# A four-layer graph network: the fourth layer's first products in one bf16 pass, its range sums by bf16 thirds, its vector products in one operation

## The chip, the core and the metric

One core of a Trainium2 chip runs the whole network in one launch. The metric is the device time of that launch in microseconds (us), the median of several runs. Before the change it is 19,167.42 us (three runs, 19,167.29 to 19,172.29).

## What is computed

The network has 12,500 nodes with 32 features (8 scalars and 8 vectors of 3) and 400,000 edges, sorted by target. Each of four layers normalizes the node features, sends messages along the edges and adds what arrives at each target to the features. The change concerns the fourth layer:

```python
h = jax.nn.relu(edge_scalars @ (fc_w1 * (1.0 / np.sqrt(NUM_BASIS)))) * SQRT2      # 8 -> 256
w = (h @ (fc_w2 * (1.0 / np.sqrt(HIDDEN)))).reshape(E, 4, MUL, MUL)               # 256 -> 4 x 8 x 8
x = node_features[edge_src]
s1 = x[:, :MUL]
v1 = x[:, MUL:].reshape(E, MUL, 3)
s2 = edge_sh[:, 0]
v2 = edge_sh[:, 1:4]
out_s = A_SCALAR * (jnp.einsum('eu,euw->ew', s1 * s2[:, None], w[:, 0]) + INV_SQRT3 * jnp.einsum('eui,ei,euw->ew', v1, v2, w[:, 1]))
out_v = A_VECTOR * INV_SQRT3 * (jnp.einsum('eu,euw,ei->ewi', s1, w[:, 2], v2) + jnp.einsum('eui,euw->ewi', v1 * s2[:, None, None], w[:, 3]))
edge_features = jnp.concatenate([out_s, out_v.reshape(E, 3 * MUL)], axis=1)
node_out = jax.ops.segment_sum(edge_features, edge_dst, num_segments=N)
```

Every edge has a small network of its own scalars (8, then 256, then 256 values), whose result weights the features of the edge's source; the weighted sums are added up by target.

## The kernel before

The edges are cut into windows of 2,048: 16 columns of 128 edges, 196 windows in all. Since the edges are sorted by target, the targets of a window span fewer than 128 nodes, so the sums of a window form one tile of 128 nodes by 32 features (this is the path named fast; another one, for inputs where that does not hold, is chosen at run time and not taken here). Layer 0 runs from 0 to about 5.1 ms, layers 1 and 2 together from 5.15 to 16.23 ms, and the fourth layer, `edges3`, from 16.33 to 23.06 ms. Beside layer 0's groups a generator, `rest`, is stepped: it clears the tables, prepares the weights and computes some values by edge.

`edges3` is unrolled over the 196 windows. For a window `c` and four quarters `s` of four columns each:

- `fetch` (called two windows ahead) loads the sources, the places of the targets, `edge_attr_4` and the eight scalars (`emb`, four transfers on SP), and issues 16 gathers on POOL (L1130), one for each column, of the source features `hs`.
- `hidden` (L1140, one window ahead) makes the 256 hidden values: two f32 matmuls for each quarter, with 8 contracted rows and 512 edges each, and a relu on ACT (L1142).
- `scalars` (L1149 to L1152) forms the two scalar inputs `q` on DVE.
- `product` (L1162) makes the 256 weights of each edge: eight matmuls a quarter with 128 hidden rows. An f32 matmul is recorded as two passes. Then DVE multiplies out of PSUM: `pa` (L1167, 512 elements) and four times `pb` (L1172, 256 elements each).
- `places` makes the one-hot matrix `oh` of each column on ACT (L1194, L1195).
- `outputs` (L1178 to L1188), for the window before, reduces `pa` and `pb` on DVE, multiplies by `edge_attr_4` and adds, into `f` (32 values an edge).
- `collect` (L1201) sums `f` by target with 16 f32 matmuls; four columns run in four column groups of PE, so four partial sums of 32 rows come out. ACT copies them (L1204), and `add` folds the four into one (L1207), which ACT copies (L1209) and `put` writes to one of two tables (SP).

Each engine works off its own list in order. The lists follow the Python code, but a scheduler may let an instruction pass others: PE takes, after a quarter's product, collect of the window before, then hidden, fold and the other quarters between them; DVE takes the two large reduces ahead of the next window's quarter 0. The PSUM tiles of the weights (`pw3`) have two buffers, so PE can be two quarters ahead of DVE. At the end `gather_sum` adds the tables (two for this layer) to the features.

Of the kernel before, what the change touches and what calls it, by code (L numbers as in the profile page):

```python
# [16 lines left out]
P = 128  # L17
# [9 lines left out]
NTAB = 4  # L27
ROUND = 12582912.0
# [7 lines left out]
class GNN:  # L36
# [14 lines left out]
    def __init__(self, tc, ctx, a, out, E):  # L51
# [15 lines left out]

        self.mid = dram.tile([rows, D + 1], F32, name="mid", tag="mid")
# [10 lines left out]
    def setup(self):  # L79
# [48 lines left out]
        self.w1q = keep.tile([P, 256], F32, name="w1q")  # L128
        self.w2b = keep.tile([P, 2, 256], F32, name="w2b")

    def weights(self, pool):
# [47 lines left out]
        nc.vector.memset(self.w1q, 0.0)  # L179
        for q in range(Q4):  # L180
            nc.scalar.dma_start(self.w1q[32 * q : 32 * q + 8], self.a["L3_gnn_fc_w1"])
        nc.vector.tensor_scalar_mul(self.w1q, self.w1q, math.sqrt(2.0) / math.sqrt(8.0))
# [14 lines left out]
    def rest(self, pool):  # L197
# [4 lines left out]
        for l in range(4):  # L202
            for t in self.tabs[l][:2] if self.fast and l != 2 else self.tabs[l]:
                self.clear(t, zero)
                yield
        yield from self.weights(pool)
        if self.fast:
            yield from self.places_by_edge(pool)
            yield from self.unit_vectors(pool)

# [100 lines left out]

    def clear(self, t, zero):
# [50 lines left out]
    def gather_sum(self, l, pool):  # L363
# [3 lines left out]
        for k, t in enumerate(self.tabs[l][: 2 if self.fast and l != 2 else NTAB]):  # L367
# [22 lines left out]

    def get(self, pool, l, c):
# [4 lines left out]
    def put(self, l, c, s):  # L396

        self.nc.sync.dma_start(self.tabs[l][c["no"] % 2][ds(self.first(c), P), :], s)

# [699 lines left out]
    def layer3(self):  # L1099
        nc = self.nc  # L1100
        self.norm_relu(3)
# [5 lines left out]
    def edges3(self):  # L1107

        nc, tc, CT = self.nc, self.tc, self.CT
        IT = CT * CPI1  # L1110
        with ExitStack() as ctx:
            ld = ctx.enter_context(tc.tile_pool(name="load3", bufs=2))
# [6 lines left out]
            def fetch(c, it):  # L1119
                row = it * CPI1 + c["no"]  # L1120
                c["src"] = self.load(gp, "src", c["col"])
                c.update(self.places_of(gp, row))
                c["sh"] = self.load(gp, "edge_attr_4", c["col"])
                c["emb"] = ld.tile([P, B], F32, name="emb")
                for q in range(Q4):
                    nc.sync.dma_start(c["emb"][32 * q : 32 * q + 8],
                                      self.a["ea8_c"][q, :, ds(row, 1), :].rearrange("f o e -> f (o e)"))
# [6 lines left out]
            def hidden(c, m, h):  # L1134
                if (m, h) == (0, 0):
                    c["hid"] = wp.tile([P, 2, CT, Q4, 32], F32, name="hid")
                t = ph.tile([P, 2, B], F32, name="ps_h")
                for q in range(2):
                    r = 32 * (2 * h + q)
                    nc.tensor.matmul(t[:, q, :], lhsT=self.w1q[r : r + 8, m * P : (m + 1) * P],  # L1140
# [248 lines left out]
```

## Time and profile before

| what | value |
|---|---|
| median of three runs | 19,167.42 us |
| the profiled execution | 23,109.4 us |
| its span on the chip | 23,107.7 us |
| mean granted TensorE clock in it | 0.828 of full |
| recorded instructions | 229,565 |
| DMA packets | 1,503,407 |

The profile is of one execution in which every instruction and packet was recorded; it took 3,942 us longer than the median of the runs. PE is TensorE's matmuls, PEld its weight loads, DVE VectorE, ACT ScalarE, POOL GpSimd (which issues the gathers) and SP the engine that issues most transfers. In a row of groups there are the line, the engine, the operation, output and inputs with their shapes and the count, then busy time in us with the mean of one in ns, then the idle time of the engine just before, with what ended it; "issue" means that the engine waited for nothing that the profile shows.

```profile
PE 15954.9 (69%) x74484; PEld 8493.8 (37%) x74484; DVE 11868.8 (51%) x24410; ACT 5515.5 (24%) x12954; POOL 14407.0 (62%) x12552
L1130 POOL DMA_INDIRECT hs<-feat,src x3136 | 3085.0, 984 | 3653.4 <-DVE pb L1172 2657.8
L1162 PE MATMUL ps_w<-w2b,hid 128*128 128x256 f32 x12544 | 4006.1, 462 | 608.6 <-issue 430.0
L1140 PE MATMUL ps_h<-emb,w1q 8*128 8x512 f32 x3136 | 1066.5, 761 | 230.0 <-DMA emb<-in_ea_c 165.1
L1172 DVE TENSOR_TENSOR pb<-ps_w,hs 128x256 f32<-128x256 f32 x3136 | 1281.8, 469 | 0.0
```

Over the whole span PE has the most busy time. In the fourth layer its largest group is the products of L1162.

### The profile page before, as it was taken

What the parts mean: (1) busy time and instruction counts of PE and PEld (TensorE: products, weight loads), DVE (VectorE), ACT (ScalarE), POOL (GpSimd) and SP (SyncE); (2) the same over time, 40 slices, a digit from 0 to 9 for tenths busy, and PEclk for the clock granted to TensorE, in tenths of its full rate; (3) what the DMA queues carried; (4) which work ended last, traced back from release to release, by engine and by line L of the source; (5) the groups of instructions that cost most, each with busy time, mean ns of one, the idle gap of its engine ahead of it and who ended that gap; (6) DMA issues with size and microseconds to landing.
All of it is one profiled execution on the core that took longest, in us unless ns stands there. A gap on an engine that the chain in (4) does not pass through costs nothing.

```text
span 23107.7 us, 229565 instructions
## 1 busy us (share of the span) xinstructions
PE 15954.9 (69%) x74484; PEld 8493.8 (37%) x74484; DVE 11868.8 (51%) x24410; ACT 5515.5 (24%) x12954; POOL 14407.0 (62%) x12552
## 2 busy tenths in 40 slices
PE   2333333328888778778777777787588888888887
PEld 2333333322333333333333333333355445445544
DVE  4443333335555555555555555555455555555555
ACT  0000000002222222222222222222233333333333
POOL 5666666655777777777777777777444444444443
PEclk9999999998777777777777777777687888888887
DMA  2111111113333333333333333333100000000000
GB/s 74 42 35 23 23 23 23 23 40 73 80 80 79 77 78 83 77 78 82 80 78 81 80 77 79 78 83 77 24 12 12 12 12 12 12 12 12 12 12 18
DMA packets 1503407, 1138.52 MB, mean 49 GB/s; under 512 B 1141492, under 2 KB 1304900, under 8 KB 1448308
## 3 DMA queue, kind: packets, MB, share of 16 engines
q1 hardware_dynamic: 745098, 891.46, 12.3%
q0 software_dynamic: 752640, 206.32, 9.7%
q10 hardware_dynamic: 4448, 25.89, 0.3%
q8 instruction: 592, 9.70, 0.2%
q14 instruction: 629, 5.15, 0.1%
HBM read 1022.56 MB, written 99.86 MB: 49 GB/s over the span
## 4 chain that ended last, share of the span: by engine, by line
PE 39%; DVE 18%; another core or an unknown queue 15%; issue 11%; ACT 9%; POOL 5%; DMA 2%; DVEq 0%; SPq 0%; POOLq 0%; ACTq 0%
PE ps_y L746 11%; PE ps_w L1162 10%; PE ps_o L756 4%; PE ps L879 4%; ACT oh L781 3%; DVE z L749 3%; DVE rb L1180 3%; POOL hs L433 2%; DVE pb L1172 2%; PE ps_h L1140 2%; ACT oh L710 2%; PE ps_win L385 2%; PE ps_sum L1201 1%; DVE f L1178 1%
## 5 line engine op out<-in xcount | busy, mean ns | idle before, releaser
L885 POOL DMA_INDIRECT acc<-summed,rows x3136 | 4995.6, 1593 | 1898.0 <-issue 1141.3
L1130 POOL DMA_INDIRECT hs<-feat,src x3136 | 3085.0, 984 | 3653.4 <-DVE pb L1172 2657.8
L1162 PE MATMUL ps_w<-w2b,hid 128*128 128x256 f32 x12544 | 4006.1, 462 | 608.6 <-issue 430.0
L433 POOL DMA_INDIRECT hs<-feat,src x3136 | 3136.5, 1000 | 1881.0 <-issue 864.2
L704 POOL DMA_INDIRECT hs<-feat,src_c x3136 | 3189.0, 1017 | 1126.7 <-issue 932.0
L1162 PEld LDWEIGHTS ps_w<-w2b,hid 128*128 128x128 f32 x12544 | 2722.3, 227 | 2283.9 <-issue 1572.6
L749 DVE TENSOR_TENSOR z<-ps_y,hid 128x1024 f32<-128x1024 f32 x2352 | 2842.0, 1218 | 1235.5 <-PE ps_y L746 1007.3
L385 PE MATMUL ps_win<-m,oh 128*128 128x32 f32 x6272 | 1488.0, 402 | 2521.3 <-ACT m L561 1829.8
L746 PE MATMUL ps_y<-X,w2t 64*128 64x512 f32 x4704 | 2258.9, 838 | 613.4 <-ACT hid L741 306.4
L385 PEld LDWEIGHTS ps_win<-m,oh 128*128 128x128 f32 x6272 | 1398.1, 328 | 2612.4 <-ACT m L561 1921.6
L1167 DVE TENSOR_TENSOR pa<-ps_w,q 128x512 f32<-128x512 f32 x784 | 536.0, 684 | 3153.4 <-PE ps_w L1162 2928.4
L756 PE MATMUL ps_o<-z,sums 128*32 128x512 f32 x9408 | 1936.9, 697 | 2.5 <-issue 1.6
L746 PE MATMUL ps_y<-Q,w2t 64*128 64x512 f32 x4704 | 1688.5, 740 | 83.6 <-DVE z L749 39.8
L723 PE MATMUL ps_m<-eye,hs 128*32 128x128 f32 x6272 | 805.2, 367 | 1048.3 <-ACT X L729 790.5
L879 PEld LDWEIGHTS ps<-hd,eq 128*128 128x128 f32 x6272 | 1048.0, 253 | 1241.9 <-issue 339.4
L879 PE MATMUL ps<-hd,eq 128*128 128x32 f32 x6272 | 1144.2, 335 | 513.7 <-DVE eq L871 197.1
L732 DVE TENSOR_TENSOR Q<-N,X 128x512 f32<-128x512 f32 x392 | 271.6, 693 | 2115.6 <-ACT X L729 1473.0
L1142 ACT ACTIVATE hid<-ps_h 128x1024 f32<-128x1024 f32 x784 | 799.8, 1020 | 2236.2 <-PE ps_h L1140 1651.5
L1172 DVE TENSOR_TENSOR pb<-ps_w,hs 128x256 f32<-128x256 f32 x3136 | 1281.8, 469 | 0.0
L1140 PE MATMUL ps_h<-emb,w1q 8*128 8x512 f32 x3136 | 1066.5, 761 | 230.0 <-DMA emb<-in_ea_c 165.1
L746 PEld LDWEIGHTS ps_y<-X,w2t 64*128 64x128 f32 x4704 | 603.4, 236 | 1658.0 <-issue 742.6
L723 PEld LDWEIGHTS ps_m<-eye,hs 128*32 128x32 f32 x6272 | 546.2, 147 | 1635.2 <-ACT X L729 929.7
(191 smaller groups left out, 18563.7 us busy)
## 6 DMA issues: line engine op xcount, KB each, us to landing
has<-loc_t SPq DMA_DIRECT2D x392, 1024.0 KB
srow<-in_src_t SPq DMA_DIRECT2D x392, 512.0 KB
hs<-feat,src POOLq DMA_INDIRECT x6272
N<-n_t SPq DMA_DIRECT2D x3136, 32.0 KB
edge_attr<-in_edge_attr SPq DMA_DIRECT2D x196, 256.0 KB
hs<-feat,src_c POOLq DMA_INDIRECT x3136
acc<-summed,rows POOLq DMA_INDIRECT x3136
emb<-in_ea_c SPq DMA_DIRECT2D x784, 20.0 KB
```

Source lines behind the costliest of these rows:

```text
L385: nc.tensor.matmul(c["sum"], lhsT=oh[:, k, :], rhs=feat[:, k, :], start=t0 + k == 0, stop=t0 + k == self.CT - 1)
L433: self.nc.gpsimd.indirect_dma_start(out=t[:, k, :], out_offset=None, in_=self.feats[l][:], in_offset=bass.IndirectOffsetOnAxis(ap=idx[:, t ...
L704: nc.gpsimd.indirect_dma_start(out=c["hs"][:, k, :], out_offset=None, in_=self.feats[1][:], in_offset=bass.IndirectOffsetOnAxis(ap=c["src_ ...
L746: nc.tensor.matmul(y[:, q, :], lhsT=self.w2t[64 * q : 64 * q + 64, j, :], rhs=c["Q" if j < 3 else "X"][64 * q : 64 * q + 64, h, :], start= ...
L749: nc.vector.tensor_mul(z, y, c["hid"][:, 2 * h : 2 * h + 2, :])
L756: nc.tensor.matmul(c["o", j // 3][32 * q : 32 * q + 32, :], lhsT=self.sums[:, j, :], rhs=c["z", j, q // 2][:, q % 2, :], start=j % 3 == 0, ...
L879: nc.tensor.matmul(t[:, k, :], lhsT=c["eq"][:, k, :], rhs=c["hd"][:, G * g + k, :], start=True, stop=True)
L885: nc.gpsimd.indirect_dma_start(out=self.tabs[2][k % NTAB][:], out_offset=bass.IndirectOffsetOnAxis(ap=c["rows"][:, G * g + k : G * g + k + ...
L1130: nc.gpsimd.indirect_dma_start(out=c["hs"][:, k, :], out_offset=None, in_=self.feats[3][:], in_offset=bass.IndirectOffsetOnAxis(ap=c["src" ...
L1140: nc.tensor.matmul(t[:, q, :], lhsT=self.w1q[r : r + 8, m * P : (m + 1) * P], rhs=c["emb"][r : r + 8], start=True, stop=True)
L1162: nc.tensor.matmul(w[:, k, :], lhsT=c["hid"][:, m, 4 * g + k].rearrange("p q s -> p (q s)"), rhs=self.w2b[:, m, :], start=m == 0, stop=m == 1)
L1172: nc.vector.tensor_mul(c["pb"][:, i, gs], w[:, :, lo : lo + 64].rearrange("p g (w u) -> p g w u", u=8), by[:, :, None, :].to_broadcast([P, ...
```

## The change

- **First products.** The eight edge scalars are split into three bf16 parts each, whose sum is the f32 value, once for all windows (`parts_of`, stepped in `rest` beside layer 0): each part is written three times to a new tensor in HBM, `emb8`, 57.8 MB in bf16. The weights are split likewise (`stacked`), so that one bf16 matmul with 72 contracted rows makes all nine products of parts. `emb` comes in one transfer of 72 rows by 2,048 edges.
- **Range sums.** `f` is split into three bf16 parts (`thirds`: two copies on ACT, two subtracts on DVE, in turn), `oh` is bf16, and `collect` is 16 bf16 matmuls with 96 columns of weights, one after another, a quarter later than before; the fold runs over 96 rows.
- **Vector products.** The features are stored with the vector components outermost, `vv` holds them multiplied by the scalar of `edge_attr_4`, and `product` makes `pa`, `ps` (256 elements) and `pv` (768 elements, the three components in one operation). `outputs` reduces `pa`, `pv` and `ps`.
- **Around these.** Loads are four windows ahead in six buffers, gathers two ahead as before; the loop of one pass is dropped; `put_late` writes the sums from ACT's queue, with the row number loaded there, to one of four tables instead of two.

```diff
+TABS = {0: 2, 1: 2, 2: 4, 3: 4}
...
+        self.emb8 = dram.tile([9, 8, self.NW, Q4 * B], BF16, name="emb8", tag="emb8")
...
-        self.w1q = keep.tile([P, 256], F32, name="w1q")
+        self.w1s = keep.tile([72, 256], BF16, name="w1s")
...
-        nc.vector.memset(self.w1q, 0.0)
-        for q in range(Q4):
-            nc.scalar.dma_start(self.w1q[32 * q : 32 * q + 8], self.a["L3_gnn_fc_w1"])
-        nc.vector.tensor_scalar_mul(self.w1q, self.w1q, math.sqrt(2.0) / math.sqrt(8.0))
+        self.stacked(pool, self.w1b, self.w1s)
...
-            for t in self.tabs[l][:2] if self.fast and l != 2 else self.tabs[l]:
+            for t in self.tabs[l][: TABS[l]] if self.fast else self.tabs[l]:
...
+            yield from self.parts_of(pool, self.a["ea8_c"], self.emb8)
...
+    def parts_of(self, pool, src, dst):
+        nc = self.nc
+        flat = src.rearrange("f c e -> (f c e)").rearrange("(p e) -> p e", p=P)
+        outs = [dst[k].rearrange("f c e -> (f c e)").rearrange("(p e) -> p e", p=P) for k in range(9)]
+        F = flat.shape[1] // 14
+        for k in range(0, flat.shape[1], F):
+            ks = slice(k, k + F)
+            v = pool.tile([P, 2240], F32, name="pv", bufs=2)[:, :F]
+            nc.sync.dma_start(v, flat[:, ks])
+            yield
+            p = [pool.tile([P, 2240], BF16, name=f"pp{i}")[:, :F] for i in range(3)]
+            nc.scalar.copy(p[0], v)
+            nc.vector.tensor_tensor(v, v, p[0], op=ALU.subtract)
+            yield
+            nc.scalar.copy(p[1], v)
+            nc.vector.tensor_tensor(p[2], v, p[1], op=ALU.subtract)
+            for i in range(3):
+                for j in range(3):
+                    nc.sync.dma_start(outs[3 * i + j][:, ks], p[i])
+            yield
+    def stacked(self, pool, w, out):
+        nc = self.nc
+        f, m = w.shape
+        p = pool.tile([f, 3, m], BF16, name="wp")
+        r = pool.tile([f, m], F32, name="wr")
+        nc.vector.tensor_copy(p[:, 0], w)
+        nc.vector.tensor_tensor(r, w, p[:, 0], op=ALU.subtract)
+        nc.vector.tensor_copy(p[:, 1], r)
+        nc.vector.tensor_tensor(p[:, 2], r, p[:, 1], op=ALU.subtract)
+        for i in range(3):
+            for j in range(3):
+                k = (3 * i + j) * f
+                nc.scalar.dma_start(out[k : k + f], p[:, j])
...
-        for k, t in enumerate(self.tabs[l][: 2 if self.fast and l != 2 else NTAB]):
+        for k, t in enumerate(self.tabs[l][: TABS[l] if self.fast else NTAB]):
...
+    def thirds(self, pool, c, step):
+        nc = self.nc
+        if step == 0:
+            c["f3"] = pool.tile([P, self.CT, 3, D], BF16, name="f3")
+        if step % 2 == 0:
+            nc.scalar.copy(c["f3"][:, :, step // 2, :], c["f"])
+        elif step == 1:
+            nc.vector.tensor_tensor(c["f"], c["f"], c["f3"][:, :, 0, :], op=ALU.subtract)
+        else:
+            nc.vector.tensor_tensor(c["f3"][:, :, 2, :], c["f"], c["f3"][:, :, 1, :], op=ALU.subtract)
...
+    def put_late(self, l, c, s):
+        first = self.nc.values_load(c["wbase"], engines=[mybir.EngineType.Activation], min_val=0, max_val=self.N - 1)
+        self.nc.scalar.dma_start(self.tabs[l][c["no"] % TABS[l]][ds(first, P), :], s)
...
-        self.norm_relu(3)
+        self.norm_relu(3, by_part=self.fast)
...
-            ld = ctx.enter_context(tc.tile_pool(name="load3", bufs=2))
+            ld = ctx.enter_context(tc.tile_pool(name="load3", bufs=6))
...
-            def fetch(c, it):
-                row = it * CPI1 + c["no"]
-                c["src"] = self.load(gp, "src", c["col"])
-                c.update(self.places_of(gp, row))
-                c["sh"] = self.load(gp, "edge_attr_4", c["col"])
-                c["emb"] = ld.tile([P, B], F32, name="emb")
-                for q in range(Q4):
-                    nc.sync.dma_start(c["emb"][32 * q : 32 * q + 8],
-                                      self.a["ea8_c"][q, :, ds(row, 1), :].rearrange("f o e -> f (o e)"))
+            def fetch(c):
+                row = c["no"]
+                c["src"] = self.load(ld, "src", c["col"])
+                c.update(self.places_of(ld, row))
+                c["sh"] = self.load(ld, "edge_attr_4", c["col"])
+                c["emb"] = ld.tile([72, Q4 * B], BF16, name="emb")
+                nc.sync.dma_start(c["emb"], self.emb8[:, :, ds(row, 1), :].rearrange("k f o e -> (k f) (o e)"))
+            def gather(c):
                 c["hs"] = gp.tile([P, CT, D], F32, name="hs")
                 for k in range(CT):
                     nc.gpsimd.indirect_dma_start(
                         in_offset=bass.IndirectOffsetOnAxis(ap=c["src"][:, k : k + 1], axis=0))
...
-                    r = 32 * (2 * h + q)
-                    nc.tensor.matmul(t[:, q, :], lhsT=self.w1q[r : r + 8, m * P : (m + 1) * P],
-                                     rhs=c["emb"][r : r + 8], start=True, stop=True)
+                    e0 = (2 * h + q) * B
+                    nc.tensor.matmul(t[:, q, :], lhsT=self.w1s[:, m * P : (m + 1) * P],
+                                     rhs=c["emb"][:, e0 : e0 + B], start=True, stop=True)
...
-                dd = wp.tile([P, CT, 8, 3], F32, name="dd", bufs=1)
-                nc.vector.tensor_mul(dd, vec, sh[:, :, None, 1:4].to_broadcast([P, CT, 8, 3]))
-                nc.vector.tensor_reduce(q[:, :, 8:16], dd, AX.X, ALU.add)
+                dd = wp.tile([P, CT, 3, 8], F32, name="dd", bufs=1)
+                nc.vector.tensor_mul(dd, hs[:, :, 8:32].rearrange("p g (k u) -> p g k u", k=3),
+                                     sh[:, :, 1:4, None].to_broadcast([P, CT, 3, 8]))
+                nc.vector.tensor_reduce(q[:, :, 8:16], dd.rearrange("p g k u -> p g u k"), AX.X, ALU.add)
+                vv = c["vv"] = wp.tile([P, CT, 3, 8], F32, name="vv")
+                nc.vector.tensor_mul(vv.rearrange("p g i u -> p g (i u)"), hs[:, :, 8:32], sh[:, :, 0:1].to_broadcast([P, CT, 24]))
...
-                    c["pb"] = wp.tile([P, 4, CT, 8, 8], F32, name="pb")
+                    c["ps"] = wp.tile([P, CT, 8, 8], F32, name="ps")
+                    c["pv"] = wp.tile([P, CT, 3, 64], F32, name="pv")
...
-                for i in range(4):
-                    lo = 128 if i == 0 else 192
-                    by = hs[:, :, 0:8] if i == 0 else vec[:, :, :, i - 1]
-                    nc.vector.tensor_mul(c["pb"][:, i, gs], w[:, :, lo : lo + 64].rearrange("p g (w u) -> p g w u", u=8),
-                                         by[:, :, None, :].to_broadcast([P, 4, 8, 8]))
+                nc.vector.tensor_mul(c["ps"][:, gs], w[:, :, 128:192].rearrange("p g (w u) -> p g w u", u=8),
+                                     hs[:, :, None, 0:8].to_broadcast([P, 4, 8, 8]))
+                nc.vector.tensor_mul(c["pv"][:, gs].rearrange("p g i (w u) -> p (g i) w u", u=8),
+                                     w[:, :, None, 192:256].to_broadcast([P, 4, 3, 64]),
+                                     c["vv"][:, gs].rearrange("p g i u -> p (g i) u")[:, :, None, :].to_broadcast([P, 12, 8, 8]))
             def outputs(c):
                 sh = c["sh"]
                 f = c["f"] = wp.tile([P, CT, D], F32, name="f")
+                fv = f[:, :, 8:32]
                 nc.vector.tensor_reduce(f[:, :, 0:8], c["pa"], AX.X, ALU.add)
-                rb = wp.tile([P, 4, CT, 8], F32, name="rb", bufs=1)
-                nc.vector.tensor_reduce(rb.rearrange("p i g w -> p (i g) w"),
-                                        c["pb"].rearrange("p i g w u -> p (i g) w u"), AX.X, ALU.add)
-                fv = f[:, :, 8:32].rearrange("p g (w k) -> p g w k", k=3)
+                nc.vector.tensor_reduce(fv.rearrange("p g (w i) -> p g i w", i=3),
+                                        c["pv"].rearrange("p g i (w u) -> p (g i) w u", u=8), AX.X, ALU.add)
+                rs = wp.tile([P, CT, 8], F32, name="rs", bufs=1)
+                nc.vector.tensor_reduce(rs, c["ps"], AX.X, ALU.add)
                 t1 = wp.tile([P, CT, 8, 3], F32, name="t1", bufs=1)
-                nc.vector.tensor_mul(t1, rb[:, 0, :, :, None].to_broadcast([P, CT, 8, 3]),
+                nc.vector.tensor_mul(t1, rs[:, :, :, None].to_broadcast([P, CT, 8, 3]),
                                      sh[:, :, None, 1:4].to_broadcast([P, CT, 8, 3]))
-                nc.vector.tensor_mul(fv, rb[:, 1:4].rearrange("p i g w -> p g w i"),
-                                     sh[:, :, 0:1, None].to_broadcast([P, CT, 8, 3]))
-                nc.vector.tensor_add(fv, fv, t1)
+                nc.vector.tensor_add(fv, fv, t1.rearrange("p g w i -> p g (w i)"))
...
-                    c["oh"] = wp.tile([P, CT, P], F32, name="oh")
+                    c["oh"] = wp.tile([P, CT, P], BF16, name="oh")
...
-                    j = 32 * (k % 4)
-                    nc.tensor.matmul(c["sum"][j : j + 32, 0:P], lhsT=c["f"][:, k, :], rhs=c["oh"][:, k, :],
-                                     start=k < 4, stop=k >= CT - 4)
-                c["s4"] = wp.tile([P, P], F32, name="s4")
-                nc.scalar.copy(c["s4"], c["sum"][:, 0:P])
+                    nc.tensor.matmul(c["sum"][: 3 * D, 0:P], lhsT=c["f3"][:, k].rearrange("p i f -> p (i f)"), rhs=c["oh"][:, k, :],
+                                     start=k == 0, stop=k == CT - 1)
+                c["s4"] = wp.tile([3 * D, P], F32, name="s4")
+                nc.scalar.copy(c["s4"], c["sum"][: 3 * D, 0:P])
             def add(c):
-                nc.tensor.matmul(c["sum"][:, P : P + D], lhsT=c["s4"], rhs=self.fold, start=True, stop=True)
-                s = wp.tile([P, D], F32, name="wsum")
+                nc.tensor.matmul(c["sum"][:, P : P + D], lhsT=c["s4"], rhs=self.fold[: 3 * D], start=True, stop=True)
+                s = wp.tile([P, D], F32, name="wsum", bufs=4)
                 nc.scalar.copy(s, c["sum"][:, P : P + D])
-                self.put(3, c, s)
-            with tc.For_i(0, self.NW // CPI1, 1) as it:
-                i = it * IT
-                cs = [{"no": c, "col": i + c * CT} for c in range(CPI1)]
-                fetch(cs[0], it)
-                fetch(cs[1], it)
+                self.put_late(3, c, s)
+            NW = self.NW
+            cs = [{"no": c, "col": c * CT} for c in range(NW)]
+            for c in range(4):
+                fetch(cs[c])
+            for c in range(2):
+                gather(cs[c])
+            for s in range(4):
+                hidden(cs[0], s % 2, s // 2)
+            scalars(cs[0])
+            for c in range(NW + 1):
+                now = cs[c] if c < NW else None
+                if c + 4 < NW:
+                    fetch(cs[c + 4])
+                if c + 2 < NW:
+                    gather(cs[c + 2])
                 for s in range(4):
-                    hidden(cs[0], s % 2, s // 2)
-                scalars(cs[0])
-                for c in range(CPI1 + 1):
-                    now = cs[c] if c < CPI1 else None
-                    if c + 2 < CPI1:
-                        fetch(cs[c + 2], it)
-                    for s in range(4):
-                        if now:
-                            product(now, s)
-                            places(now, 4 * s, 4 * s + 4)
-                        if c and s == 0:
-                            outputs(cs[c - 1])
-                        if c and s == 1:
-                            collect(cs[c - 1])
-                        if c and s == 2:
-                            add(cs[c - 1])
-                        if c + 1 < CPI1:
-                            hidden(cs[c + 1], s % 2, s // 2)
-                            if s == 3:
-                                scalars(cs[c + 1])
+                    if now:
+                        product(now, s)
+                        places(now, 4 * s, 4 * s + 4)
+                    if c:
+                        last = cs[c - 1]
+                        if s == 0:
+                            outputs(last)
+                            self.thirds(wp, last, 0)
+                        elif s == 1:
+                            self.thirds(wp, last, 1)
+                            self.thirds(wp, last, 2)
+                        elif s == 2:
+                            self.thirds(wp, last, 3)
+                            collect(last)
+                        else:
+                            add(last)
+                    if c + 1 < NW:
+                        hidden(cs[c + 1], s % 2, s // 2)
+                        if s == 3:
+                            scalars(cs[c + 1])
...
-    data["ea8_c"] = e["edge_attr_8"].reshape(NW, Q4, B, 8).transpose(1, 3, 0, 2)
+    data["ea8_c"] = e["edge_attr_8"].reshape(NW, C, 8).transpose(2, 0, 1)
```

More of the change, by code (lines that the diff above doesn't have):

```diff
@@ L1109, in edges3 @@
         nc, tc, CT = self.nc, self.tc, self.CT
-        IT = CT * CPI1
         with ExitStack() as ctx:
-            ld = ctx.enter_context(tc.tile_pool(name="load3", bufs=2))
+            ld = ctx.enter_context(tc.tile_pool(name="load3", bufs=6))
             gp = ctx.enter_context(tc.tile_pool(name="gather3", bufs=4))
@@ L1146, in scalars @@
                 hs, sh = c["hs"], c["sh"]
-                vec = hs[:, :, 8:32].rearrange("p g (u k) -> p g u k", k=3)
                 q = c["q"] = wp.tile([P, CT, 16], F32, name="q")
                 nc.vector.tensor_mul(q[:, :, 0:8], hs[:, :, 0:8], sh[:, :, 0:1].to_broadcast([P, CT, 8]))
-                dd = wp.tile([P, CT, 8, 3], F32, name="dd", bufs=1)
-                nc.vector.tensor_mul(dd, vec, sh[:, :, None, 1:4].to_broadcast([P, CT, 8, 3]))
-                nc.vector.tensor_reduce(q[:, :, 8:16], dd, AX.X, ALU.add)
+                dd = wp.tile([P, CT, 3, 8], F32, name="dd", bufs=1)
[4 more added lines that the diff above has]
+                nc.vector.tensor_mul(vv.rearrange("p g i u -> p g (i u)"), hs[:, :, 8:32], sh[:, :, 0:1].to_broadcast([P, CT, 24]))
             def product(c, g):
@@ L1165, in product @@
                 hs = c["hs"][:, gs, :]
-                vec = hs[:, :, 8:32].rearrange("p g (u k) -> p g u k", k=3)
                 nc.vector.tensor_mul(c["pa"][:, gs], w[:, :, 0:128].rearrange("p g (w u) -> p g w u", u=16),
                                      c["q"][:, gs, None, :].to_broadcast([P, 4, 8, 16]))
-                for i in range(4):
-                    lo = 128 if i == 0 else 192
-                    by = hs[:, :, 0:8] if i == 0 else vec[:, :, :, i - 1]
-                    nc.vector.tensor_mul(c["pb"][:, i, gs], w[:, :, lo : lo + 64].rearrange("p g (w u) -> p g w u", u=8),
-                                         by[:, :, None, :].to_broadcast([P, 4, 8, 8]))
+                nc.vector.tensor_mul(c["ps"][:, gs], w[:, :, 128:192].rearrange("p g (w u) -> p g w u", u=8),
[3 more added lines that the diff above has]
+                                     c["vv"][:, gs].rearrange("p g i u -> p (g i) u")[:, :, None, :].to_broadcast([P, 12, 8, 8]))
             def outputs(c):
```

## The prediction

> **What bounds the kernel now.** I began with the page's shares, then cut the span into its stages and went to the fourth layer, where almost all of the change lies.
>
> ```profile
> span 23107.7 us, 229565 instructions
> PE   2333333328888778778777777787588888888887
> DVE  4443333335555555555555555555455555555555
> POOL 5666666655777777777777777777444444444443
> PEclk9999999998777777777777777777687888888887
> ```
>
> Slices 29 to 40 are the fourth layer (16.33 to 23.06 ms): PE looks like the bound, DVE is half busy, and the granted clock is often below full. The windows view shows more. Here are one window of 2,048 edges from the middle of the layer and one of the last two, for which POOL has no gathers left (columns: stretch, length, busy PE, PEld, DVE, ACT, POOL with counts, clock, DMA share, GB/s):
>
> ```profile
> 20024.89:20059.00 34.11, 27.57 (x114) 16.95 (x114) 17.97 (x29) 12.08 (x27) 15.75 (x17) 0.85 0.07 12
> 22991.17:23012.92 21.75, 20.49 (x114) 14.05 (x114) 18.01 (x29) 11.64 (x26) 0.00 (x0) 1.00 0.01 1
> ```
>
> The same 114 matmul passes and the same DVE work take 34.1 us with gathers and 21.75 without. The timeline of PE says where the 12.35 us go; first the window with gathers, then the one without:
>
> ```profile
> 20027.17 0.27 PE L1201 MATMUL ps_sum<-oh,f 128*32 128x128 f32 x1 [1.11 <-issue]
> 20027.89 0.27 PE L1201 MATMUL ps_sum<-oh,f 128*32 128x128 f32 x1 [0.45 <-issue]
> 20030.72 3.68 PE L1162 MATMUL ps_w<-w2b,hid 128*128 128x256 f32 x7 [0.92 <-issue]
> 20038.15 2.08 PE L1140 MATMUL ps_h<-emb,w1q 8*128 8x512 f32 x4
> 20040.16 5.82 PE L1162 MATMUL ps_w<-w2b,hid 128*128 128x256 f32 x16
> ```
>
> ```profile
> 22991.17 1.08 PE L1201 MATMUL ps_sum<-oh,f 128*32 128x128 f32 x32 [0.52 <-DVE f L1188]
> 22992.18 2.86 PE L1162 MATMUL ps_w<-w2b,hid 128*128 128x256 f32 x12
> 22995.11 1.13 PE L1140 MATMUL ps_h<-emb,w1q 8*128 8x512 f32 x4
> 22996.17 3.72 PE L1162 MATMUL ps_w<-w2b,hid 128*128 128x256 f32 x16
> ```
>
> With gathers, after the burst of 32 collect passes PE issues one instruction per some 0.7 us, for "issue", that is for nothing the profile shows; collect to fold takes about 13 us instead of 3.7. The clock then falls to half and the next products run at 5.82 instead of 3.72 us.
>
> **Is that stall there when nothing is recorded?** The profiled execution took 23,109.4 us, 2 more than its span, but the median of the runs is 19,167.42: 3,942 us of the profile are missing from the runs. 193 windows with gathers at 12.35 us too long are 2,384 of these; the other 1,558 would then come from the first three layers, where POOL leaves 0.30 us after each of 9,408 gathers, 2,820 us in all. So I read the stall as one of recording, and the run's period as 21.75 us. [...] The rows alone do not settle it: if the first layers lost all 2,820 us, only 1,122 would be left for the fourth, and its true period would be 28.4. [...]
>
> **The fourth layer, part by part.** Costs are those of the window without gathers.
>
> ```profile
> 23002.09 2.27 DVE L1178 TENSOR_REDUCE f<-pa 128x128 f32<-128x2048 f32 x1
> 23004.29 4.41 DVE L1180 TENSOR_REDUCE rb<-pb 128x512 f32<-128x4096 f32 x1
> 23008.62 0.68 DVE L1167 TENSOR_TENSOR pa<-ps_w,q 128x512 f32<-128x512 f32 x1
> 23009.21 1.62 DVE L1172 TENSOR_TENSOR pb<-ps_w,hs 128x256 f32<-128x256 f32 x4
> 2002.60 0.64 PE L585 MATMUL ps_deg<-olo,ohi 128*125 128x100 bf16 x4
> ```
>
> Hidden: f32 costs two passes; four take 1.06 us start to start. One bf16 pass each halves it: four times 0.53, PE −2.1 us per window.
> Collect: 32 f32 passes at 0.87 us [...] become 16 bf16 pairs one after another. The row of L585 gives (0.64 − 0.31) / 3 = 0.11 us a pair at 100 columns; at 128 between 0.08 and 0.13: 1.3 to 2.0, taken 1.6. PE +0.7, so PE's sum falls from 19.2 to about 17.8.
> Vector products: four operations, 1.57 us start to start, become one of 256 (0.40) and one of 768 elements (0.88 by the slope of L1167 to L1172, where 256 more elements cost 0.2 to 0.3; three times L1172's 0.40 would be 1.2, three times that slope alone 0.7): −0.29 a quarter, −1.15 per window, between +0.1 and −1.9. A quarter is now 0.60 + 0.40 + 0.88 = 1.88 us of DVE. The reduce of 4,096 splits into 3,072 (3.27) and 1,024 (1.14): +0.1. One multiply of 384 goes, one (vv, 0.47) comes. Thirds on DVE: two subtracts of 512, 0.6 each by L1167: +1.2. DVE's sum stays at 18.0.
> Thirds on ACT: two copies of about 0.6, and the put with its load of the row number (SP's row for L402 is 0.51 + 0.15 us) moves from SP to ACT. ACT goes from 11.6 to 13.6 of 24 us, covered by PE's and DVE's chain; behind the load stands a relu of hid, which PE needs only a window part later. Uncovered it would be 0.7. SP issues one emb transfer instead of four (0.35 us each), 295 KB instead of 64 KB per window: 12 GB/s more, fetched four windows ahead. The trace has one wait of PE for emb in the whole layer, at its start (165 us, for the first loads), so there is nothing to gain in the windows, and with DMA 7% busy nothing to lose; ends ±0.3 us. The loop that goes had one pass: nothing. POOL keeps its 16 gathers of 0.95 + 0.30 us = 19.9, under both periods.
>
> The sums are not the period; the order is. In the built program DVE's order per window is: products of quarter 3, q, vv, both reduces of f, products of the next window's quarter 0, rs, quarter 1 with t1 and the add, the first subtract, quarter 2, the last subtract; only then may collect begin, and on PE quarter 3's product stands behind collect, hidden and fold. So nothing overlaps there: 1.88 + 0.57 + 0.47 + 2.20 + 3.27 = 8.4; + 1.9 + 1.14 + 2.85 (a quarter, t1 0.46, the add 0.50) + 0.6 + 1.9 + 0.6 = 17.4 us of DVE; PE has by then done its other quarters (at about 13.9) and idles 3.6 us. Then collect 1.6, two hidden passes beside PE to ACT to PE 0.74 (the copy of the sum), fold 0.25, quarter 3's product 3.45, 0.31 back to DVE: 23.7 us. Before, collect waited 0.52 us for the add, and PE was the bound at 20.5 of 21.75. What PE's fewer passes free is given up to the new wait[...]. The unsure ends of this chain: collect ±0.35, the 768-element multiply four times from −0.2 to +0.3[...]: 22.3 to 25.3.
>
> **The clock.** A window row at half clock has the products 2.1 us longer. [...] Always halved for collect and the product it costs up to 2.5 us (26.3), by the row without gathers, where PE idles 0.52 us before collect and the clock is 1.00, nothing (23.7). I take +0.8: **24.5 us**, +2.75 on 21.75, over 195 windows +536 us.
>
> **Elsewhere.** Splitting emb in layer 0: 14 chunks, each one load, 9 writes of 459 KB on SP, two copies of 1,792 elements on ACT and two subtracts on DVE (about 2 us each), stepped between layer 0's groups. 57.8 MB at the page's rate for that queue (891 MB in 12.3% of the span, 313 GB/s) are 185 us of the DMA engines; hidden behind POOL's gathers at best (0), all exposed 185; taken 30, as POOL has 0.5 to 0.6 busy slices there. Two more copies in the norm 3.5 us; two more tables summed at the end, by the third layer's, which has four, 16 + 7 us; longer tail 3. Together +60.
>
> Predicted: 19,167 + 536 + 60 = **19,760 us**. In the profile's own time it may look the other way: PE's burst shrinks from 228 recorded instructions a window to 180, so period 34.1 may fall to 25 to 28 and the span to about 21,600, with the median up.
>
> **The rivals.**
> *The stall is partly real* (faster, 0.30). Place: PE after collect. It speaks for it that POOL fills 91% of layers two and three (8,089 us busy and 2,046 of its 0.30-us gaps, of some 11,080), so these may have lost more than 1,558 us. Price: at the profile's ratio of 0.829 the true period is 28.3; after, with fewer passes, 24.7: 19,167 − 3.6 × 195 + 60 = 18,520. It decides from a true period of 24.8 on. *All of it is real* (0.06): 34.1 to 26, 17,650; against it stands the 3,942 us sum.
> *The clock stays half through collect and product* (0.13): 26.5 us, 20,150[...].
> *The thirds are hidden* (0.05), ACT and DVE finish before PE, period unchanged: 19,230; against it: the 17.4 us chain.
>
> **Numbers.** Slower as worked out 0.46, its own range 19,450 to 20,050 (period 23.2 to 26). Cases: 0.46 + 0.13 + 0.02 slower, 0.03 within 0.2% (38 us, what a measurement can tell from no change), 0.36 faster. The range reaches from the first rival, 18,400, to the third, 20,150.
>
> **What would show it.** After's last windows, without gathers: 23.5 to 26 us, PE idle over 3 us before collect, released by the last subtract; right. A period under 22 there: the chain is wrong. [...] A profile shorter by 1,500 us and a median higher: the stall was recording. A median under 18,900: it was real. Layer 0 over 100 us longer: the split is exposed.

## The result, and the profile after

The kernel after takes 18,951.36 us (median of four, 18,939.83 to 18,958.99), before 19,167.35 (four runs): ratio 0.9887, 95% interval 0.9875 to 0.9898. It is faster by 216 us, where slower by 593 was forecast.

The kernel before took about 19,100 us in some sets of runs ("the 19,100 level", that of the result) and 23,200 to 23,500 in others ("the 23,200 level", that of the page ahead of the prediction), with all runs of a set alike, so kernels are compared below by their ratio to before in the same set.

The page of after (19,100 level), its rows as before; in the last rows out<-in, count, busy us, mean ns, idle us and releaser:

```profile
span 18938.1 us, 218835 instructions
PE   3444444446888888888888888888885688888887
DVE  4555444446666666666666666666665688888887
POOL 5777777776888888888888888888887677777775
PEclk9999999999777777777777777777776899999998
L1184 POOL DMA_INDIRECT hs<-feat,src x3136 | 3093.7, 987 | 1057.9 <-issue 909.1
L1220 PE MATMUL ps_w<-w2b,hid 128*128 128x256 f32 x12544 | 3008.5, 393 | 84.9 <-DVE pv L1228 84.7
```

The row of the products in before, recorded at the same level (before_third, below):

```profile
L1162 PE MATMUL ps_w<-w2b,hid 128*128 128x256 f32 x12544 | 3118.7, 398 | 173.8 <-DVE pb L1172 173.8
```

So PE's idle time before the products falls from 173.8 to 84.9 us, and neither has the "issue" of the page ahead of the prediction. Of POOL's 1,057.9 us of idle time 909.1 are its own gap between gathers. The timeline of a window (PE, then DVE):

```profile
16806.87 3.62 PE L1220 MATMUL ps_w<-w2b,hid 128*128 128x256 f32 x16
16813.57 1.86 PE L1256 MATMUL ps_sum<-oh,f 128*96 128x128 bf16 x16 [3.09 <-DVE f L439]
16816.35 4.50 PE L1220 MATMUL ps_w<-w2b,hid 128*128 128x256 f32 x18
```

```profile
16812.82 0.69 DVE L439 TENSOR_TENSOR f<-f,f 128x512 bf16<-128x512 f32 x1 [4.18 <-ACT f L435]
16814.10 0.68 DVE L1224 TENSOR_TENSOR pa<-ps_w,q 128x512 f32<-128x512 f32 x1
16816.86 2.28 DVE L1236 TENSOR_REDUCE f<-pa 128x128 f32<-128x2048 f32 x1
```

After its last subtract (L439) DVE goes on with `q` and then a quarter's `pa`, without waiting for PE, and reduces `pa` 2 us later. The reduce needs all four quarters, so that quarter is the last, and its product is the row of 16 passes *ahead* of collect. The forecast had it behind.

The last windows of the same execution, for which POOL has no gathers left, decide between the two orders (PE, then DVE):

```profile
18818.78 3.62 PE L1220 MATMUL ps_w<-w2b,hid 128*128 128x256 f32 x16
18822.23 1.06 PE L1256 MATMUL ps_sum<-oh,f 128*96 128x128 bf16 x16
```

```profile
18807.40 2.28 DVE L1236 TENSOR_REDUCE f<-pa 128x128 f32<-128x2048 f32 x1
18822.43 0.69 DVE L1224 TENSOR_TENSOR pa<-ps_w,q 128x512 f32<-128x512 f32 x1 [0.18 <-PE ps_w L1220]
18825.21 2.28 DVE L1236 TENSOR_REDUCE f<-pa 128x128 f32<-128x2048 f32 x1
```

Collect follows the last quarter's product with no idle time of PE, DVE waits 0.18 us, and the window is 17.81 us. The prediction had named 23.5 to 26 us there as its sign of being right, and a period under 22 as the sign that its chain is wrong.

### The profile page after: what moved, and what is told of

Same layout as the page of the kernel before. It is cut to its first block, busy times and chain, and to the rows that moved or that the text cites. A ratio compares the mean times of both kernels' runs of the same rounds, so it can differ in the third digit from the quotient of the medians.

```text
span 18938.1 us, 218835 instructions
## 1 busy us (share of the span) xinstructions
PE 14058.8 (74%) x69780; PEld 7931.9 (42%) x69780; DVE 11912.7 (63%) x23464; ACT 5816.6 (31%) x13374; POOL 14614.9 (77%) x12552
## 4 chain that ended last, share of the span: by engine, by line
PE 31%; POOL 23%; DMA 14%; DVE 14%; issue 9%; ACT 8%; SPq 0%; ACTq 0%; another core or an unknown queue 0%; DVEq 0%; POOLq 0%
PE ps_y L801 13%; DMA hs<-feat,src 10%; POOL hs L488 7%; POOL hs L1184 7%; PE ps_o L811 5%; POOL hs L759 5%; PE ps L934 4%; POOL acc L940 4%; ACT oh L836 3%; DVE z L804 2%; DVE f L1237 2%; ACT oh L765 2%; PE ps_m L778 2%; DMA hs<-feat,src_c 2%; DVE f L1236 1%
## 5 line engine op out<-in xcount | busy, mean ns | idle before, releaser
L759 POOL DMA_INDIRECT hs<-feat,src_c x3136 | 3299.4, 1052 | 1048.9 <-issue 887.2
L488 POOL DMA_INDIRECT hs<-feat,src x3136 | 3215.9, 1025 | 1063.8 <-issue 750.0
L1184 POOL DMA_INDIRECT hs<-feat,src x3136 | 3093.7, 987 | 1057.9 <-issue 909.1
L1220 PE MATMUL ps_w<-w2b,hid 128*128 128x256 f32 x12544 | 3008.5, 393 | 84.9 <-DVE pv L1228 84.7
L1220 PEld LDWEIGHTS ps_w<-w2b,hid 128*128 128x128 f32 x12544 | 2434.0, 197 | 565.8 <-DVE pv L1228 133.1
L801 PE MATMUL ps_y<-X,w2t 64*128 64x512 f32 x4704 | 2108.8, 793 | 143.4 <-ACT hid L796 122.4
L801 PE MATMUL ps_y<-Q,w2t 64*128 64x512 f32 x4704 | 1764.9, 766 | 44.4 <-DVE z L804 42.5
L615 DVE TENSOR_TENSOR m<-hs,edge_attr 128x128 f32<-128x128 f32 x784 | 238.9, 305 | 1967.4 <-DMA hs<-feat,src 1951.0
L616 ACT ACTIVATE m<-m 128x128 f32<-128x128 f32 x784 | 242.5, 309 | 3482.8 <-DVE m L615 2183.4
L936 ACT COPY summed<-ps 128x128 f32<-128x128 f32 x784 | 208.6, 266 | 3540.1 <-PE ps L934 3263.5
L1250 ACT ACTIVATE oh<-iota,local 128x128 bf16<-128x128 f32 x3136 | 1057.3, 391 | 48.8 <-DMA local<-local 26.2
```

The lines of the kernel that those rows point to most:

```text
L488: self.nc.gpsimd.indirect_dma_start(out=t[:, k, :], out_offset=None, in_=self.feats[l][:], in_offset=bass.IndirectOffsetOnAxis(ap=idx[:, t ...
L759: nc.gpsimd.indirect_dma_start(out=c["hs"][:, k, :], out_offset=None, in_=self.feats[1][:], in_offset=bass.IndirectOffsetOnAxis(ap=c["src_ ...
L801: nc.tensor.matmul(y[:, q, :], lhsT=self.w2t[64 * q : 64 * q + 64, j, :], rhs=c["Q" if j < 3 else "X"][64 * q : 64 * q + 64, h, :], start= ...
L1184: nc.gpsimd.indirect_dma_start(out=c["hs"][:, k, :], out_offset=None, in_=self.feats[3][:], in_offset=bass.IndirectOffsetOnAxis(ap=c["src" ...
L1220: nc.tensor.matmul(w[:, k, :], lhsT=c["hid"][:, m, 4 * g + k].rearrange("p q s -> p (q s)"), rhs=self.w2b[:, m, :], start=m == 0, stop=m == 1)
L1250: nc.scalar.activation(c["oh"][:, k, :], self.iota, AF.Square, bias=c["local"][:, k : k + 1], scale=-1.0)
```

## The experiments

Fourteen runs, with the change itself beside them. "Window" is the mean distance between two starts of the reduce into `f`, over the fourth layer.

| run | before beside it, us | time, us | ratio, 95% interval | window, us |
|---|---|---|---|---|
| before_third | 19,109 | 19,131 | (one run) | 22.07 |
| hidden_alone_2 | 19,109 | 18,864 | 0.9871 (0.9854 to 0.9887) | 20.59 |
| thirds_alone_2 | 19,109 | 19,381 | 1.0144 (1.0127 to 1.0161) | 23.31 |
| after_without_thirds | 19,109 | 18,831 | 0.9857 (0.9840 to 0.9873) | 20.34 |
| hidden_and_vectors | 19,085 | 18,806 | 0.9854 (0.9838 to 0.9871) | 20.29 |
| hidden_and_thirds | 19,085 | 18,865 | 0.9883 (0.9866 to 0.9899) | 20.64 |
| the change itself | 19,167 | 18,951 | 0.9887 (0.9875 to 0.9898) | 20.68 |
| before_again | 23,186 | 23,194 | 0.9996 (0.9974 to 1.0019) | 33.98 |
| hidden_alone | 23,186 | 22,728 | 0.9803 (0.9775 to 0.9830) | 31.68 |
| vectors_alone | 23,186 | 23,123 | 0.9971 (0.9956 to 0.9985) | 33.69 |
| thirds_alone | 23,186 | 22,726 | 0.9807 (0.9783 to 0.9831) | 32.01 |
| after_again | 23,538 | 22,125 | 0.9405 (0.9364 to 0.9447) | 27.47 |
| after_put_sp | 23,538 | 22,270 | 0.9462 (0.9424 to 0.9501) | 27.88 |
| before_no_gathers | 23,538 | 21,030 | (one run) | 21.99 |
| after_no_gathers | 23,538 | 20,150 | (one run) | 17.80 |

**Before, recorded again** (no edit).

> The kernel before, unchanged, for a second profile. Theory A (its first profiled execution was an odd one, and PE's stall under gathers is not there otherwise): span within 100 us of the 19,167 median, about 22.3 us per window of the fourth layer, that is about 4,380 us for it, and PE busy nearly all of it. Theory B (recording stalls this kernel whenever it is recorded): span about 23,100 again, windows of 34 us, while the kernel after is not slowed by its recording.

> The kernel before once more, for a profile on the chip of these runs. Where it takes some 19,100 us: Theory A: PE does not stall under gathers there, the window of the fourth layer is 22.0 to 22.6 us, with PE busy nearly throughout and POOL waiting for buffers; collect to fold about 3.7 us. Theory B (my first rival): the stall is there in part, windows of 24 us or more and gaps of 0.7 us between PE's instructions. Where it takes some 23,200: windows of 34 us, as seen.

The one set gave 34 us windows and 23,194 us, the other 22.07 and 19,131. Both were recorded in the same way. So recording alone does not bring the stall of PE. In the first run theory A falls, and the second run refutes the first's theory B (a stall whenever this kernel is recorded); its own theory A holds. The windows view of before at the 19,100 level, with gathers (columns as in the prediction):

```profile
15000.00:18500.00 3500.00, 3324.76 (x18062) 2282.61 (x18061) 2858.09 (x4434) 1844.89 (x4118) 2511.82 (x2537) 0.98 0.12 19
```

PE is busy 95%, DVE 82%, POOL 72% (92% with its own gaps). The timeline has two waits of PE in a window of 21.75 us and one long one of DVE, which waits for PE:

```profile
16818.14 3.69 PE L1162 MATMUL ps_w<-w2b,hid 128*128 128x256 f32 x16 [0.74 <-DVE pb L1172]
16828.76 1.08 PE L1201 MATMUL ps_sum<-oh,f 128*32 128x128 f32 x32 [0.53 <-DVE f L1188]
16829.77 2.86 PE L1162 MATMUL ps_w<-w2b,hid 128*128 128x256 f32 x12
```

```profile
16837.51 0.69 DVE L1167 TENSOR_TENSOR pa<-ps_w,q 128x512 f32<-128x512 f32 x1 [2.60 <-PE ps_w L1162]
```

These are the rows of the window without gathers. PE is the bound, and 21.75 us was the right start for the forecast.

**The first products alone** (on before; with the splitting and the stacked weights):

```diff
...
-                    nc.tensor.matmul(t[:, q, :], lhsT=self.w1q[r : r + 8, m * P : (m + 1) * P],
-                                     rhs=c["emb"][r : r + 8], start=True, stop=True)
+                    nc.tensor.matmul(t[:, q, :], lhsT=self.w1s[:, m * P : (m + 1) * P],
+                                     rhs=c["emb"][:, e0 : e0 + B], start=True, stop=True)
...
```

> Before, with only the first products in one bf16 pass (and the splitting beside layer 0). Theory A (before is bound by PE at about 22.3 us per window, after by POOL's gathers at 20.7): PE's sum falls by 2.1 us, so the window falls to POOL's 20.5 to 21: -1.5 x 196 = -290, with 30 to 60 for the splitting: about 18,920, all of the change's gain. Theory B (the later collect of the range sums is what freed PE): less than a third of the gain, above 19,100.

> Before with only the first products in one bf16 pass, once more. Where before takes 19,100 us, Theory A (PE is the bound there, POOL at 20.3 next): window 20.3 to 20.8, ratio 0.984 to 0.988, at least as much as the whole change (0.989). Theory B (PE is not the bound): ratio above 0.994. Where before takes 23,200: 0.98, as seen.

At the 19,100 level this part alone gives 0.9871, all that the change gives. The windows fall from 22.07 to 20.59, -1.48 x 195 = -289 us. Layer 0, from its first gather to that of layer 1, grows from 4,210 to 4,275 us by the splitting, and starts 18 us sooner. Together that is -242 us; the times differ by 245. What takes over as the bound is seen in POOL's row, first of before_third, then of hidden_alone_2, over the same 3,500 us:

```profile
L1130 POOL DMA_INDIRECT hs<-feat,src x2537 | 2512.2, 990 | 988.2 <-issue 716.8 <-DVE pb L1172 263.5 <-DMA hs<-feat,src 7.9
```

```profile
L1164 POOL DMA_INDIRECT hs<-feat,src x2733 | 2668.0, 976 | 833.0 <-issue 811.6 <-DVE q L1186 14.6 <-DMA hs<-feat,src 4.9
```

In before POOL waited 263.5 us for DVE to free a buffer; with the first products shortened, all its waits other than the gap are some 21. The rest of POOL's time is gathers and its own gap: 16 x (0.976 + 0.30) = 20.4 us of the 20.59. At the 23,200 level the first run fell short of its theory A (31.7 us instead of 20.5 to 21), since PE's stall is still there: its waits for "issue" are 629 us between 17,000 and 22,500, 753 in before_again.

**The vector products alone** (on before: `ps`, `pv`, `vv` and the features by component):

```diff
...
-                    nc.vector.tensor_mul(c["pb"][:, i, gs], w[:, :, lo : lo + 64].rearrange("p g (w u) -> p g w u", u=8),
-                                         by[:, :, None, :].to_broadcast([P, 4, 8, 8]))
...
+                nc.vector.tensor_mul(c["pv"][:, gs].rearrange("p g i (w u) -> p (g i) w u", u=8),
+                                     w[:, :, None, 192:256].to_broadcast([P, 4, 3, 64]),
+                                     c["vv"][:, gs].rearrange("p g i u -> p (g i) u")[:, :, None, :].to_broadcast([P, 12, 8, 8]))
...
```

> Before, with only the vector products in one operation and the features stored by component. Theory A (PE bound): DVE's sum falls by about 1.2 us a window, the time stays within 40 us of 19,167. Theory B (DVE's products hold back PE through the two PSUM buffers): -0.6 to -1.2 us a window, 18,930 to 19,050.

0.9971: 62 us of 23,186, short of theory B's 120 and beyond theory A's 40, though by the interval 35 us are possible. Without gathers its last windows take 21.23 us, 0.5 less than before's. While PE is the bound, less work on DVE is worth little. Alone, this part was not run at the 19,100 level.

**The range sums by thirds alone** (on before; put still from SP, two tables):

```diff
...
-                    nc.tensor.matmul(c["sum"][j : j + 32, 0:P], lhsT=c["f"][:, k, :], rhs=c["oh"][:, k, :],
-                                     start=k < 4, stop=k >= CT - 4)
+                    nc.tensor.matmul(c["sum"][: 3 * D, 0:P], lhsT=c["f3"][:, k].rearrange("p i f -> p (i f)"), rhs=c["oh"][:, k, :],
+                                     start=k == 0, stop=k == CT - 1)
...
```

> Before, with only the range sums by bf16 thirds (collect a quarter later, sums still put from SP to two tables). Theory A (PE and DVE are both near the bound): PE +0.7, DVE +1.2 us a window, the time rises by 100 to 300 us. Theory B (in before PE waits for collect, and the later place removes it): it falls by 50 to 150 us. My prediction's chain of 23.7 us, if it were right, would give at least +300.

> Before with only the range sums by thirds, once more. Where before takes 19,100 us, Theory A (quarter 3's product stands behind collect in this build, DVE waits 5.6 us for it): window 24 to 25 us, +2 x 196, ratio 1.015 to 1.03. Theory B (the late collect frees PE): ratio below 1. Where before takes 23,200: 0.98, as seen.

At the 19,100 level it is slower, 1.0144, just short of theory A of the second run (1.015 to 1.03; its window was to be 24 to 25 us, and is 23.31), and the chain of the forecast is there. PE, then DVE:

```profile
17006.29 1.09 PE L1212 MATMUL ps_sum<-oh,f 128*96 128x128 bf16 x16 [0.43 <-DVE f L401]
17008.36 5.39 PE L1174 MATMUL ps_w<-w2b,hid 128*128 128x256 f32 x16
17013.59 0.31 PE L1218 MATMUL ps_sum<-fold,s 96*128 96x32 f32 x2
```

```profile
17005.54 0.69 DVE L401 TENSOR_TENSOR f<-f,f 128x512 bf16<-128x512 f32 x1
17013.79 0.69 DVE L1179 TENSOR_TENSOR pa<-ps_w,q 128x512 f32<-128x512 f32 x1 [4.94 <-PE ps_w L1174]
```

Here the product with which DVE ends the window stands behind collect, and DVE is idle 4.94 us for it. The window is 24.0 us (this one) or 22.4 (most). At the 23,200 level the same kernel is faster, 0.9807, and theory A of that run fell. That PE's burst is 32 recorded instructions with the thirds, for the 64 in which it stalls in before, fits this, but is not shown to be the cause: hidden_alone keeps the burst of 64 and gains as much (0.9803).

**Two parts together.**

> Before with the first products in one bf16 pass and the vector products in one operation, the range sums as in before (f32, 32 passes in one burst). Theory A (thirds pay by shortening PE's burst, and only on a chip that stalls PE under gathers): last windows without gathers 18 to 19 us, as good as after; on a chip that stalls, windows with gathers about 31.5 us, as with the first products alone, against 27.3 of after, ratio 0.975 to 0.985. Theory B (the thirds pay by themselves): last windows 20 us or more.

> Before with the first products in one bf16 pass and the range sums by thirds, the vector products as in before. Theory A (with the first products shortened, DVE is the bound when POOL is not, and quarter 3's product goes ahead of collect): last windows 19.1 us, DVE's sum, 1.3 more than after; with gathers on a chip that stalls 27.5 to 29 us. Theory B (the chain of collect ahead of quarter 3's product comes with the thirds): last windows 23 us or more, as with the thirds alone.

Both ran at the 19,100 level. With the thirds and the first products together the chain is gone: quarter 3's product stands ahead of collect again, and the last windows, without gathers, take 19.05 us, DVE's sum, as theory A said; with the first products and the vector products they take 18.3. With gathers all these kernels stand at 20.3 to 20.7 us, whatever PE and DVE save below that. Why the built order differs where the thirds stand alone stays open.

**After without thirds** (collect in f32 in four column groups and a quarter earlier, all else as in after).

> After with the range sums as in before (f32 in four column groups, a quarter earlier), all else of the change kept: loads four windows ahead, put from ACT, four tables. Where before takes 19,100 us: POOL at 20.3 us is the bound, so as the two parts on before (0.985), or 0.980 to 0.984 if its waits for loads (180 us for edge_attr there) were on the path. Theory B (thirds needed): above 0.989. Where before takes 23,200: 0.955 to 0.98, against 0.94 of after, since the burst is 64 instructions again.

0.9857, with hidden_and_vectors (0.9854) the best of all. Theory B falls: at this level the thirds are not needed, and the two kernels without them are some 0.3% below the change's 0.9887. They ran in other sets than the change's own pair, and the intervals only just part. Whether they hold at the 23,200 level was not tried.

**Without gathers, and the put.**

> Before, with gathers for the first two windows of the fourth layer alone (all later windows read these again, so its sums are other ones). Theory A (PE's stall comes only with gathers): the window is 21.7 us throughout, as in the last windows of before, and PE is the bound. Theory B (it has another cause): 28 us or more.

> After, with gathers for the first two windows of the fourth layer alone. Theory A (DVE is its bound when POOL is not, and quarter 3's product is done before collect): 17.8 us per window, the sum of DVE's work, on any chip. My prediction's chain: 23.7 us or more.

```diff
+                if c["no"] >= 2:
+                    c["hs"] = cs[c["no"] % 2]["hs"]
+                    return
```

In both kernels every window from the third on leaves out its gathers and reads the features of the first two again. At the 23,200 level that gives 22.0 and 17.8 us: PE's stall goes with the gathers, and after's own work needs 17.8. Its view over 2,000 us:

```profile
17000.00:19000.00 2000.00, 1939.03 (x10107) 1540.93 (x10106) 1979.68 (x2588) 1430.35 (x3140) 0.00 (x0) 1.00 0.08 21
```

DVE is busy 99%, the clock is 1.00: no chain, no halved clock.

> The kernel after, unchanged, on the chip of these runs. On a chip where before takes some 23,190 us PE stalls after a burst of instructions while POOL gathers. Theory A (the stall grows with the instructions that PE issues): after has 48 of 228 fewer in a window and a burst of 32 instead of 64, its window falls from 34.3 to 26 to 29 us and the time by 5 to 8%. Theory B (the stall is tied to the gathers alone): its window stays above 32 us, the time falls by 2% at most. Where before takes 19,170 us: 18,950.

Theory A: at the 23,200 level the whole change gives 0.9405, window 27.47, with 180 recorded PE instructions a window for 228. The prediction's aside on the profile's own time (a period of 25 to 28, a span of about 21,600) came near: the span is 22,055 us, but the median fell with it.

> After, with the load of the row number and the put of the sums on SP's queue as in before, instead of ACT's. Theory A (POOL sets after's window at 20.7 us): within 40 us of after. Theory B (ACT's wait at its load of the row number, 440 us in after's fourth layer, delays the thirds and with them collect): faster by 100 us or more. Theory C (SP's wait for the sums holds back its loads): slower by 50 us or more.

145 us above after by the medians, which fits theory C, but the two intervals overlap; it is not faster, so theory B falls at this level.

## Why the prediction was wrong, by its own steps

- **"I read the stall as one of recording, and the run's period as 21.75 us."** The number was right (21.75 the median window of before_third), the reason was not: the stall comes and goes between sets of runs that are recorded alike. That recording holds back PE was my assumption; no run shows it. The first rival, a stall that is partly real, gave the right sign by luck: the 19,100 level does not have its mechanism.
- **"On PE quarter 3's product stands behind collect, hidden and fold."** This is the step that failed. I read one product too few ahead of collect: PE works a quarter ahead of DVE, and the one just before collect is quarter 3's. So after L439 DVE has its input; the 6.3 us that I added behind the 17.4 of DVE (collect, copy, fold, product, hand-over) run beside q, `pa`, `ps`, `pv` and the reduces. The window of after is 17.8 us instead of 23.7 where nothing else binds. The chain does exist where the thirds stand alone on before, at 22.4 to 24.0 us.
- **"PE idle over 3 us before collect, released by the last subtract; right".** This was to be seen in the windows without gathers, and there PE does not idle before collect at all. With gathers something like it is seen, 3.09 us, but not from the forecast's chain: DVE's last subtract waited 4.18 us for ACT's second copy, which stood behind the load of the row number (on ACT 5.23 us of waiting for the transfer of `local`, the load at 16,810.7, the copy at 16,812.18). The prediction had that load at 0.7 us if uncovered.
- **"DVE's sum stays at 18.0."** 17.8; right.
- **"POOL keeps its 16 gathers ... = 19.9, under both periods."** In after a gather takes 0.987 us and its gap 0.30: 20.6, 0.7 more, and it is *over* after's 17.8: the bound. With the order read rightly, the forecast's own 19.9 against 21.75 would have given -1.85 x 195 + 60 = -301 us, and 20.6 gives -164; measured -216. The windows themselves fell from 22.07 to 20.68, -271 us in all.
- **Hidden, 4 x 0.53, and collect, 1.6 us.** Without gathers hidden takes 0.43 to the next start (17,002.09 to 17,002.52), four times 1.7, and collect 0.89 (17,005.98 to 17,006.87). Both were over-sized, without effect, as PE is not the bound.
- **The clock, +0.8 us.** This was my estimate between nothing and 2.5 us, the latter partly from a row of 5.82 us whose mean clock is 0.63 (before, 20,040.16 to 20,046.00). Without gathers the granted clock is 1.00 (after_no_gathers, 17,000 to 19,000 us), with them 0.95 (after, 15,000 to 18,700). In the window shown PE idles 3.09 us; then the clock is 0.52 over collect, hidden and fold (16,813.57 to 16,816.35), and collect takes 1.86 us for 1.06 without gathers. In the next window PE idles 1.54 us there, the clock is 1.00 (16,833.63 to 16,835.32) and collect takes 1.09. Where the thirds stand alone, quarter 3's product takes 5.39 us (17,008.36), where as many passes at 17,001.09 take 3.72, though PE idled only 0.43 of the 3.62 us before it. What lengthens it is not shown; the clock is 0.96 over 15,000 to 18,500 us. In after it all acts on an engine that is not the bound.
- **Elsewhere, +60.** Against before_third, layer 1's first gather comes 73 us later in after (4,368 for 4,295), 47 in hidden_alone_2 and 39 in after_without_thirds, where 30 were taken for the splitting. The norm ahead of the fourth layer takes 5 us more, and the end after the last window 29 (82 for 53), where 30 were forecast for norm, tables and tail.
- **The range.** Its low end does not follow from its period: (23.2 - 21.75) x 195 + 60 gives 19,510, not 19,450.
- **"A profile shorter by 1,500 us and a median higher"** did not come: at the 23,200 level the median fell by 1,413 us too.

## What to carry to other kernels

When one engine's list is read against another's, number the pieces on both sides (which quarter does this multiply read?) before adding durations along a chain; with two PSUM buffers the producer can be a piece ahead (in after PE starts quarter 3's product at 16,806.87, and DVE its `pa` at 16,814.10). After an engine is made faster, compare the new sum with every other engine's sum, its gaps included: here POOL at 20.4 to 20.6 us took over from PE at 21.75, and at the 19,100 level two of the three parts then bought nothing that the intervals show. Before a ratio is worked out from a profile whose time differs from the median by a fifth, suspect that it ran under another condition, and take the stage's time from a stretch that the disturbance does not reach.

## What was not expected of the hardware

- The same kernel ran at 19,109 and at 23,186 to 23,538 us. At the slower level PE, late in collect's burst of 64 recorded instructions, falls to one per 0.7 us (in before from 20,027.17 on; collect to fold takes some 13 us, the window 34), and without gathers does not (21.99). Layers 0 to 2 are longer too: layer 0 by its gathers is 5,020 us in before against 4,210 in before_third, layers 1 and 2 are 11,223 in before against 10,394 in after.
- What makes the level stays open. The sets of after_again (23,538) and hidden_alone_2 (19,109) ran on a chip of the same number. Gathers take as long at both levels (0.982 us in before_again, 0.990 in before_third), and the queue of instructions, q8, takes much the same share of the 16 DMA engines (0.2% with 132 packets in 5,000 us, 0.3% with 143 in 3,500). The slower level has waits outside PE as well: in before_again (17,000 to 22,500 us) ACT waits 1,897 us and DVE 107 for a "remote" signal that the profile cannot place, which the waits of before_third (15,000 to 18,500) do not have.
- ACT's load of the row number for the put waits for the transfer of `local` in after, which delays the second copy of the thirds. The waits view of after, 15,000 to 18,700 us (us, times, longest):

```profile
DVE f L439 <- ACT f L435: 520.1, 178, 5.1
ACT hid L1197 <- DMA local<-local: 441.1, 115, 6.1
```

What it costs at the 19,100 level is not shown; at the 23,200 level the put from SP was no faster.
- A bf16 pair of 96 columns of weights and 128 moving columns followed the next at 0.89 / 16 = 0.056 us, half of the 0.11 that the pairs of L585 showed.
